# Gather, expert, scatter: large and small experts in turns, a fixed order of POOL's transfers, and two tails in one output tile

## The chip, the cores and the metric

The kernel runs on one core of a Trainium2 chip. The metric is the time of one execution on the device in microseconds (us); lower is better. Beside the times there is a profiled execution, from which every row below is taken. Engines: PE (matrix products; PEld is its weight load), DVE (vector), ACT (activation), POOL (here it issues indirect DMA transfers), SP (issues direct transfers).

## What is computed

One graph layer over 12,500 nodes with 256 features (a mean over neighbours with two normalisations, two linear maps), a mixture of 64 experts of which each node takes two, a normalisation over nodes, and a layer norm of the sum with the input:

```python
x = gc + (feats @ W_res + b_res)
logits = x @ Wg + bg
vals, idx = jax.lax.top_k(logits, TOP_K)          # TOP_K = 2, E = 64
gates = jax.nn.softmax(vals, axis=-1)
...
h1 = jax.nn.gelu(jnp.einsum('ecd,edh->ech', h, w1) + b1[:, None, :])   # D 256 -> H 512
h2 = jnp.einsum('ech,ehd->ecd', h1, w2) + b2[:, None, :]              # H 512 -> D 256
core = jnp.zeros((N, D), x.dtype).at[tok_s].add(g_s[:, None] * y_s)
y = x + core
...
return _layernorm(x + batch_normalised(y))
```

h holds, for each expert, the rows of x of the nodes that chose it (at most 1024). All products are in float32, which PE does in two passes.

## The kernel before

Three stages follow each other: the graph layer with the choice of experts (to about 2552 us), the experts (2552 to 3434 us), and the two normalisations. The change touches the expert stage alone.

Experts are ordered by how many nodes they have, largest first, and expert number i of this order has room for TOKENS[i]×16 rows. An expert's rows are cut into **parts** of at most four tiles of 128 rows: 83 parts and 241 tiles in all. The last tile of an expert, its **tail**, is often short. The order of parts is the smallest expert (number 63), then 0, 1, 2 and so on to 62.

For part q the program goes through these steps.

- `begin(q)`: for a new expert, SP loads its weights (1 MB, tile `w`, L1614) and bias (L1616) and DVE copies its lists of slots (L1762, L1764). Then POOL issues one indirect gather a tile, `xg` (L1638), of the rows of x and of what the gate needs; 16 buffers.
- `turned(q)`: DVE computes the gates of the part's tiles from the gathered rows (L1682), PE transposes the tiles into `xtp` (L1653), and DVE copies that to `xT` (L1658).
- `hidden`: PE's first products `hp` (L1667), and ACT's gelu into `h1` (L1671).
- `outputs`: for each tile, PE's second products `yp` (L1694; four j of 128 hidden units, each in two passes; two PSUM buffers), DVE adds the bias (L1699) and multiplies by the gate (L1700) into `yo` (6 buffers), and POOL issues a scatter that adds the rows of yo to z_d in memory (L1701).

The loop over q runs `hidden(q)`, `begin(q + 3)`, `turned(q + 1)`, `outputs(q)`. PE keeps this order as written. For the other engines a scheduler orders the instructions; each engine then works through its own order, and an instruction that waits holds up those behind it. POOL's gathers and scatters share one queue of transfers. The scatters of one expert may run side by side, since no node has an expert twice; those of different experts wait for each other where they meet the same tensor.

A second pass over all experts, under a condition that holds only when an expert has more rows than its room, is skipped with this data.

Of the kernel before, what the change touches and what calls it, by code (L numbers as in the profile page):

```python
# [19 lines left out]
P = 128  # L20
# [76 lines left out]
def last_node(g):  # L97
# [12 lines left out]
]  # L110
RPE = CAP // P
NSLOT = E * RPE
WROW = 2 * H + 4 * D + 4
# [8 lines left out]
def gnn_moe_kernel(  # L122
# [697 lines left out]
    with ExitStack() as stack:  # L820
# [780 lines left out]


    with ExitStack() as stack:
        wp = stack.enter_context(tc.tile_pool(name="w", bufs=3))
        one = stack.enter_context(tc.tile_pool(name="x_one", bufs=1))
        two = stack.enter_context(tc.tile_pool(name="x_two", bufs=2))
        ps1 = stack.enter_context(tc.tile_pool(name="x_ps1", bufs=1, space=PSUM))
        ps2 = stack.enter_context(tc.tile_pool(name="x_ps2", bufs=2, space=PSUM))

        REGS = 4  # L1610

        def load(e):
            w = wp.tile([P, WROW], F32, name="w")
# [5 lines left out]
        def overfull():  # L1619
# [8 lines left out]
            V.tensor_reduce(some, room, axis=AX.X, op=ALU.add)  # L1628
            V.tensor_copy(over_n, some)

        def gather(at, m):

            xg = []
            for k in range(0, m, P):
                r = min(P, m - k)
                k //= P
                g = two.tile([P, D2], F32, name="xg", bufs=16)
                GP.indirect_dma_start(  # L1638
                    out=g[:r],
                    out_offset=None,  # L1640
                    in_=x2_d,
                    in_offset=bass.IndirectOffsetOnAxis(ap=at[:r, 0, k : k + 1], axis=0),
                )
                xg.append(g[:r])
            return xg

        def turn(xg):

            xtp = ps1.tile([P, 2, 4 * P], F32, name="xtp")
            for k, g in enumerate(xg):  # L1650
                r = g.shape[0]
                for c in range(2):
                    T.transpose(  # L1653
                        xtp[:, c, k * P : k * P + r], g[:, c * P : (c + 1) * P], ident[:r, :r]
                    )
            m = k * P + r
            xT = two.tile([P, 2, 4 * P], F32, name="xT")
            V.tensor_copy(xT[:, :, :m], xtp[:, :, :m])  # L1658
            return xT
# [25 lines left out]
                )  # L1685
            return gate

        def outputs(w, bb, at, gate, h1, m, group):
            w2 = w[:, 2 * H : 2 * H + 4 * D].rearrange("p (c d) -> p c d", d=D)
            for k in range(-(-m // P)):  # L1690
                r = min(P, m - k * P)
                yp = ps2.tile([P, D], F32, name="yp")
                for j in range(4):
                    T.matmul(  # L1694
                        yp[:r], h1[:, j, k * P : k * P + r], w2[:, j],
                        start=j == 0, stop=j == 3,
                    )
                yo = two.tile([P, D], F32, name="yo", bufs=6)
                V.tensor_add(yo[:r], yp[:r], bb[:r])  # L1699
                V.tensor_scalar_mul(yo[:r], yo[:r], gate[:r, k : k + 1])  # L1700
                st = GP.indirect_dma_start(  # L1701
                    out=z_d,
                    out_offset=bass.IndirectOffsetOnAxis(
                        ap=at[:r, 1, k : k + 1], axis=0
                    ),
                    in_=yo[:r],
                    in_offset=None,
                    compute_op=ALU.add,
                )
                if group:  # L1710
                    tc.declare_no_dep(st.ins, group=group, reason="no node has an expert twice")
                    tc.add_to_no_dep_group(group, st.ins)


        parts = []
        for i in [E - 1, *range(E - 1)]:
            n = -(-TOKENS[i] * TU // P)
            k = -(-n // 4)
            b = 0
            for j in range(k):  # L1720
                m = (n - b + k - j - 1) // (k - j)
                parts.append((i, b, min(m * P, TOKENS[i] * TU - b * P)))
                b += m
        AHEAD = 3
        xg, given = {}, {}

        def begin(q):
            i, b, m = parts[q]
            if b == 0:
                k = 0 if i == E - 1 else i % REGS  # L1730
                if k == 0:
                    n = 1 if i == E - 1 else min(REGS, E - 1 - i)
# [14 lines left out]
                    given["regs"] = regs, columns  # L1747
                regs, columns = given["regs"]
                columns_of[i] = columns[k]
                sort_slots(i, 0)  # L1750
                if q >= AHEAD:
                    sort_slots(i, 1)
                given[i] = load(regs[k])
            xg[q] = gather(table(q), m)

        columns_of = {}

        def sort_slots(i, which):

# [6 lines left out]
        def table(q):  # L1766
            i, b, m = parts[q]
            return sorted_[:, :, i * RPE + b : i * RPE + b + 4]

        def turned(q):  # L1770
            i, b, m = parts[q]
            gate[q] = gates_of(xg[q], snd_sorted[:, i * RPE + b : i * RPE + b + 4])
            return turn(xg.pop(q))

        gate = {}
        snd_sorted = one.tile([P, NSLOT], F32)
        with tc.manual_schedule(engines={mybir.EngineType.PE}):
            for q in range(AHEAD):
                begin(q)
            V.scalar_tensor_tensor(free, node, 0.0, spread, op0=ALU.is_equal, op1=ALU.mult)  # L1780
            V.tensor_tensor(slot[:, 1], free, slot[:, 0], op=ALU.add)
            for i in sorted({parts[q][0] for q in range(AHEAD)}):
                sort_slots(i, 1)
            xT = turned(0)
            for q, (i, b, m) in enumerate(parts):
                if q >= 6 and q % 4 == 2 and (q - 6) // 4 < len(LOADS):
                    t0, n = LOADS[(q - 6) // 4]
                    r = rows(t0)
                    nc.sync.dma_start(xs[:r, t0 : t0 + n], part_of(x, t0, n))
                h1 = hidden(given[i][0], xT, m)  # L1790
                if q + AHEAD < len(parts):
                    begin(q + AHEAD)
                if q + 1 < len(parts):
                    xT = turned(q + 1)
                outputs(*given[i], table(q), gate.pop(q), h1, m, f"expert{i}")
                if q == 16:
                    overfull()


        with tc.If(nc.values_load(over_n[0:1, 0:1]) > 0):  # L1800
            for a in range(NT):
                r = rows(a)
                again = two.tile([P, D], F32, name="yo", bufs=6)
                nc.sync.dma_start(again[:r], x2_d[a * P : a * P + r, :D])
                nc.sync.dma_start(z_d[a * P : a * P + r], again[:r])
            with tc.For_i(0, E, 1) as e:
                w, bb = load(e)
                at = two.tile([P, 2, RPE], I32, name="at")
                V.tensor_copy(at, slot[:, :, bass.ds(e * RPE, RPE)])
                second = two.tile([P, RPE], F32, name="second")  # L1810
                V.tensor_copy(second, snd[:, bass.ds(e * RPE, RPE)])
                for b in range(0, RPE, 4):
                    ab = at[:, :, b : b + 4]
                    g = gather(ab, 4 * P)
                    gb = gates_of(g, second[:, b : b + 4])
                    outputs(w, bb, ab, gb, hidden(w, turn(g), 4 * P), 4 * P, None)


    with ExitStack() as stack:
# [191 lines left out]
```

## Time and profile before

| | us |
|---|---|
| median of 3 runs | 3605.96 (3599.64 to 3620.2) |
| profiled execution | 3578.72 |
| its span | 3576.8 |
| PE busy | 2531.0 (71%) |
| DVE busy | 1800.6 (50%) |
| ACT busy | 798.8 (22%) |
| POOL busy | 2175.5 (61%) |

The span covers all stages; the expert stage is its last quarter but for the normalisations. A row of the timeline gives start, duration, engine, line, operation, output and inputs, and in brackets the idle time of the engine just before with what ended it ("<-DMA xg" is the landing of a gather, "<-issue" nothing that the profile shows). A row of a group gives count, busy time, mean ns of one, and idle time by what ended it. POOL's busy time is that of issuing; the transfer goes on after it.

### The profile page before, as it was taken

Reading aid. Unit: us, or ns where it says so; the run is one execution under the profiler, and the core shown is the slowest. Engines: PE = TensorE matmul, PEld = TensorE weight load, DVE = VectorE, ACT = ScalarE, POOL = GpSimd, SP = SyncE. Lnnn points to the kernel's source line nnn. Section 1 sums busy time; section 2 is a strip of 40 time slices with the busy share of each in tenths; the row PEclk is TensorE's granted clock in tenths of the full one; section 3 lists DMA queues with packets and bytes.
Section 4 is the critical chain, followed back from the end, with each engine's and each line's share of the span. In section 5 each row is a group of like instructions: output and inputs, shape, how many; then the busy total and the mean of one; then the engine's idle time right before and its main releaser. Section 6 shows DMA issues by size and latency. Waiting matters only on the chain. (4 is left out here: it accounts for less than half of the span.)

```text
span 3576.8 us, 40049 instructions
## 1 busy us (share of the span) xinstructions
PE 2531.0 (71%) x11797; PEld 1893.4 (53%) x11797; DVE 1800.6 (50%) x7368; ACT 798.8 (22%) x1975; POOL 2175.5 (61%) x2095
## 2 busy tenths in 40 slices
PE   2526075566776667676766666677699999999966
PEld 2415043455555555554555444454377876677856
DVE  3729454355555465655555435467543333333358
ACT  2416301122111122212221111111111221122246
POOL 7250776666666666666666666665367777777610
PEclk6657566778887878897878777788899999999988
DMA  8450853444554555555544444444555666676764
GB/s 259 128 189 6 309 203 95 158 145 144 143 150 146 141 147 168 146 147 157 155 144 122 142 117 122 119 135 124 159 115 122 134 135 146 155 177 173 197 196 144
DMA packets 313919, 538.03 MB, mean 150 GB/s; under 512 B 47274, under 2 KB 233102, under 8 KB 305502
## 3 DMA queue, kind: packets, MB, share of 16 engines
q0 software_dynamic: 119360, 266.30, 28.9%
q1 hardware_dynamic: 180795, 256.19, 23.0%
q10 hardware_dynamic: 13539, 12.90, 1.2%
q8 instruction: 97, 1.59, 0.2%
q14 instruction: 128, 1.05, 0.1%
HBM read 431.02 MB, written 105.28 MB: 150 GB/s over the span
## 5 line engine op out<-in xcount | busy, mean ns | idle before, releaser
L938 POOL DMA_INDIRECT ring<-h_d,src_col x1416 | 1372.4, 969 | 711.8 <-issue 387.2
L952 PE MATMUL p<-ring,o 128*128 128x258 f32 x2832 | 902.0, 450 | 213.2 <-issue 89.7
L952 PEld LDWEIGHTS p<-ring,o 128*128 128x128 f32 x2832 | 600.4, 224 | 389.2 <-issue 214.9
L930 DVE TENSOR_SCALAR o<-lane,rel 128x128 f32<-128x128 f32 x1416 | 356.1, 297 | 402.7 <-remote 160.3
L1701 POOL DMA_INDIRECT z_d<-yo,tables x241 | 375.0, 1556 | 129.8 <-issue 58.0
L1694 PE MATMUL yp<-w,h 128*128 128x256 f32 (+7 forms) x1928 | 436.3, 381 | 0.8 <-DVE tables L1762 0.8
L1667 PE MATMUL hp<-xT,w 128*128 128x384 f32 (+22 forms) x1328 | 392.3, 449 | 9.4 <-issue 9.4
L1694 PEld LDWEIGHTS yp<-w,h 128*128 128x128 f32 (+7 forms) x1928 | 336.8, 179 | 71.0 <-issue 7.6
L1638 POOL DMA_INDIRECT xg<-x_d,tables x241 | 234.3, 972 | 183.7 <-PE xtp L1653 88.2
L1671 ACT ACTIVATE h<-hp,w 128x384 f32<-128x384 f32 (+21 forms) x332 | 178.7, 539 | 682.0 <-PE hp L1667 673.1
L1667 PEld LDWEIGHTS hp<-xT,w 128*128 128x128 f32 x1328 | 248.0, 192 | 134.1 <-issue 61.0
L1506 ACT ACTIVATE again<-again,factor 128x256 f32<-128x256 f32 x180 | 82.4, 501 | 670.3 <-issue 363.2
L986 ACT COPY s<-p 128x258 f32<-128x258 f32 x118 | 43.8, 371 | 814.8 <-PE p L952 450.0
L1658 DVE COPY xT<-xtp 128x672 f32<-128x672 f32 (+21 forms) x83 | 70.8, 853 | 305.6 <-PE xtp L1653 297.2
L1699 DVE TENSOR_TENSOR yo<-yp,bb 128x256 f32<-128x256 f32 (+7 forms) x241 | 102.0, 423 | 224.1 <-PE yp L1694 154.2
L285 POOL DMA_INDIRECT early<-in_x,src_col x130 | 135.0, 1038 | 102.4 <-DMA early_d<-early 56.3
L567 PE MATMUL deg<-o_hi,o_lo 128*128 128x98 bf16 x1254 | 107.3, 254 | 122.8 <-issue 83.8
L1481 PE MATMUL q<-r_out,tables 128*128 128x98 f32 x360 | 66.8, 315 | 150.4 <-DVE tables L1489 55.9
L1027 PE MATMUL q<-ident,s 128*128 128x128 f32 x236 | 58.9, 337 | 158.0 <-DVE tables L1489 67.5
L222 DVE TENSOR_TENSOR o_hi<-lane_b,hi 128x2450 bf16<-128x2450 bf16 (+1 forms) x67 | 95.1, 1419 | 145.8 <-remote 106.2
L565 ACT ACTIVATE s_lo<-lane_b,nb 128x128 bf16<-128x128 bf16 x396 | 121.8, 388 | 192.9 <-remote 126.7
L567 PEld LDWEIGHTS <-o_lo 128*128 128x128 bf16 x1254 | 87.5, 125 | 140.1 <-issue 91.2
(367 smaller groups left out, 3503.5 us busy)
## 6 DMA issues: line engine op xcount, KB each, us to landing
w<-in_wpack SPq DMA_DIRECT2D x64, 1026.0 KB
again<-early_d SPq DMA_DIRECT2D x90, 256.0 KB
ring<-h_d,src_col POOLq DMA_INDIRECT x1416
early_d<-early SPq DMA_DIRECT2D x65, 256.0 KB
tables<-h_d SPq DMA_DIRECT2D x104, 128.0 KB
acc<-acc_d SPq DMA_DIRECT2D x14, 896.0 KB
acc<-in_x SPq DMA_DIRECT2D x12, 1024.0 KB
x_d<-y SPq DMA_DIRECT2D x47, 258.0 KB
```

The costliest lines, as they stand in the source:

```text
L285: GP.indirect_dma_start(out=t[:, c % 2], out_offset=None, in_=x, in_offset=bass.IndirectOffsetOnAxis(ap=src_col[:, MC + c : MC + c + 1], a ...
L565: S.activation(s_lo[:, i], lane_b, AF.Sign, bias=nb[:, k - k0, i : i + 1])
L567: T.matmul(deg, o_lo[:, i], o_hi[:, i], start=c + i == 0, stop=False)
L930: o_last[u] = V.tensor_scalar(o_of[u][:, j], lane, rel[:, c : c + 1], None, op0=ALU.is_equal)
L938: i = GP.indirect_dma_start(out=r[:, k, :D], out_offset=None, in_=h_d, in_offset=bass.IndirectOffsetOnAxis(ap=src_col[:, c : c + 1], axis=0),)
L952: i = T.matmul(p_of[g], o_of[v][:, n], r[:, k], start=j == 0, stop=j == GR - 1)
L1638: GP.indirect_dma_start(out=g[:r], out_offset=None, in_=x2_d, in_offset=bass.IndirectOffsetOnAxis(ap=at[:r, 0, k : k + 1], axis=0),)
L1667: T.matmul(hp[:, :m], w1[:, c, j * P : (j + 1) * P], xT[:, c, :m], start=c == 0, stop=c == 1,)
L1671: S.activation(h1[:, j, :m], hp[:, :m], AF.Gelu, bias=w[:, 2 * H + 4 * D + j : 2 * H + 4 * D + j + 1],)
L1694: T.matmul(yp[:r], h1[:, j, k * P : k * P + r], w2[:, j], start=j == 0, stop=j == 3,)
L1699: V.tensor_add(yo[:r], yp[:r], bb[:r])
L1701: st = GP.indirect_dma_start(out=z_d, out_offset=bass.IndirectOffsetOnAxis(ap=at[:r, 1, k : k + 1], axis=0), in_=yo[:r], in_offset=None, c ...
```

## The change

Four things change in the expert stage.

- **Order of experts.** Experts (or pairs, below) are sorted by their rows, and one from the large end and one from the small end are taken in turns. The weights of an expert are found by a register load for each expert, where consecutive ones came from one load of four. `w` has 4 buffers instead of 3, `yo` 10 instead of 6.
- **Pairs.** 17 pairs of experts are formed whose tails fit together into one tile of 128 rows: two tails of 33 to 64 rows (5 pairs), or one of up to 32 and one of 65 to 96 (12 pairs). The two tails' products go to one PSUM tile `yp`, in blocks of PE's columns, 64 wide in the first case and 32 wide in the second, and block by block for each j. DVE's add and multiply and POOL's scatter are still done for each tail. Of the pair's second expert the part with the tail comes first. Its scatters wait for those of the first expert.
- **POOL's order.** Gathers and scatters get dependencies that bind only the order of issue: a gather follows what was issued before it in the program, and so does a scatter, the scatters of one expert in a row being free among themselves. In a pair's step `begin(q + 3)` stands between the scatters of the two tails.
- **Tail gathers** bring at least 80 rows, and `turn` transposes and copies as many.

```diff
-        wp = stack.enter_context(tc.tile_pool(name="w", bufs=3))
+        wp = stack.enter_context(tc.tile_pool(name="w", bufs=4))
...
+        def in_order(i, group=None):
+            if "over" in issued:
+                return
+            if group is None or group != issued["group"]:
+                issued.update(group=group, before=issued["these"], these=[])
+            for j in issued["before"]:
+                tc.add_manual_dep(
+                    i.ins, j.ins.name,
+                    mybir.DependencyInfo(
+                        mybir.DependencyClass.NoSync, mybir.DependencyReason.SCHED_ONLY
+                    ),
+                    reason="gathers and scatters are issued in this order",
+                )
+            issued["these"].append(i)
...
-                r = min(P, m - k)
+                r = max(WHOLE, min(P, m - k))
...
-                GP.indirect_dma_start(
+                i = GP.indirect_dma_start(
...
+                in_order(i)
...
+        def products(yp, r, w, h1, a, j):
+            w2 = w[:, 2 * H : 2 * H + 4 * D].rearrange("p (c d) -> p c d", d=D)
+            T.matmul(yp, h1[:, j, a : a + r], w2[:, j], start=j == 0, stop=j == 3)
...
+        def add_to_nodes(yo, at, k, group):
...
+                for before in scatters.get(mate.get(group), []):
+                    tc.add_manual_dep(
+                        st.ins, before.ins.name,
+                        mybir.DependencyInfo(mybir.DependencyClass.Sync, mybir.DependencyReason.DATA),
+                        reason="a node can have both experts of a pair",
+                    )
+                scatters.setdefault(group, []).append(st)
+                in_order(st, group)
...
+        def pair_of_outputs(two_of):
+            yp = ps2.tile([P, D], F32, name="yp")
+            tails = [of[5] % P for of in two_of]
+            width = SIDE if min(tails) > BLOCK and max(tails) <= SIDE else BLOCK
+            starts = [0, max(SIDE, -(-tails[0] // BLOCK) * BLOCK)]
+            for j in range(4):
+                for start, r, (w, bb, at, gate, h1, m, group) in zip(starts, tails, two_of):
+                    for k in range(0, r, width):
+                        n = min(width, r - k)
+                        products(yp[start + k : start + k + n], n, w, h1, m - r + k, j)
+            todo = []
+            for start, r, (w, bb, at, gate, h1, m, group) in zip(starts, tails, two_of):
+                part_of_yp = slice(start, start + r)
+                yo = gated(yp[part_of_yp], r, bb[part_of_yp], gate, m // P)
+                todo.append(lambda yo=yo, at=at, m=m, group=group: add_to_nodes(yo, at, m // P, group))
+            todo[0]()
+            return todo[1]
...
+        order = [E - 1]
+        while units:
+            order += units.pop(0)
+            if units:
+                order += units.pop()
+        order.append(E - 2)
         parts = []
-        for i in [E - 1, *range(E - 1)]:
+        for i in order:
...
-                if q + AHEAD < len(parts):
+                if q not in pair_at and q + AHEAD < len(parts):
                     begin(q + AHEAD)
                 if q + 1 < len(parts):
                     xT = turned(q + 1)
-                outputs(*given[i], table(q), gate.pop(q), h1, m, f"expert{i}")
+                mine = (*given[i], table(q), gate.pop(q), h1, m, f"expert{i}")
+                if q in pair_at:
+                    rest = pair_of_outputs([kept.pop(pair_at[q]), mine])
+                    begin(q + AHEAD)
+                if q in pair_at or q in pair_at.values():
+                    if q not in pair_at:
+                        kept[q] = mine
+                    mine = (*mine[:5], m // P * P, mine[6])
+                if q in pair_at:
+                    rest()
+                    outputs(*mine)
+                else:
+                    outputs(*mine)
```

`gated` holds the add and the multiply of DVE, `add_to_nodes` the scatter, both as they were in `outputs`. SIDE is 64, BLOCK 32, WHOLE 80, and AHEAD is 3 in both kernels.

More of the change, by code (lines that the diff above doesn't have):

```diff
@@ L110, with blocks_of @@
 ]
+SIDE, BLOCK = P // 2, P // 4
+WHOLE = SIDE + 16
+def blocks_of(r):
+    return -(-r // BLOCK)
+PAIR_OF = {}
+for _k in ((2, 2), (1, 3), (1, 1)):
+    _open = []
+    for _i, _n in enumerate(TOKENS[: E - 2]):
+        _u = blocks_of(_n * TU % P)
+        if _u not in _k or _i in PAIR_OF or _i in PAIR_OF.values():
+            continue
+        _mate = [_j for _j, _v in _open if (_v, _u) in (_k, _k[::-1])]
+        if _mate:
+            PAIR_OF[_mate[0]] = _i
+            _open = [_o for _o in _open if _o[0] != _mate[0]]
+        else:
+            _open.append((_i, _u))
 RPE = CAP // P
@@ L1655, in turn @@
                     )
-            m = k * P + r
             xT = two.tile([P, 2, 4 * P], F32, name="xT")
@@ L1686, in gates_of, with gated, outputs @@
             return gate
-        def outputs(w, bb, at, gate, h1, m, group):
+        def products(yp, r, w, h1, a, j):
             w2 = w[:, 2 * H : 2 * H + 4 * D].rearrange("p (c d) -> p c d", d=D)
-            for k in range(-(-m // P)):
+            T.matmul(yp, h1[:, j, a : a + r], w2[:, j], start=j == 0, stop=j == 3)
+        def gated(yp, r, bb, gate, k):
+            yo = two.tile([P, D], F32, name="yo", bufs=YO)
+            V.tensor_add(yo[:r], yp, bb)
+            V.tensor_scalar_mul(yo[:r], yo[:r], gate[:r, k : k + 1])
+            return yo[:r]
+        def add_to_nodes(yo, at, k, group):
+            r = yo.shape[0]
+            st = GP.indirect_dma_start(
+                out=z_d,
+                out_offset=bass.IndirectOffsetOnAxis(ap=at[:r, 1, k : k + 1], axis=0),
+                in_=yo,
+                in_offset=None,
+                compute_op=ALU.add,
+            )
+            if group:
+                tc.declare_no_dep(st.ins, group=group, reason="no node has an expert twice")
+                tc.add_to_no_dep_group(group, st.ins)
+                for before in scatters.get(mate.get(group), []):
[3 more added lines that the diff above has]
+                        reason="a node can have both experts of a pair",
+                    )
+                scatters.setdefault(group, []).append(st)
+                in_order(st, group)
+        scatters = {}
+        mate = {f"expert{j}": f"expert{i}" for i, j in PAIR_OF.items()}
+        def outputs(w, bb, at, gate, h1, m, group, ks=None):
+            for k in ks or range(-(-m // P)):
                 r = min(P, m - k * P)
@@ L1693, in outputs @@
                 for j in range(4):
[L1694 to L1709, printed above, removed]
@@ L1710, in outputs @@
-                if group:
-                    tc.declare_no_dep(st.ins, group=group, reason="no node has an expert twice")
-                    tc.add_to_no_dep_group(group, st.ins)
+                    products(yp[:r], r, w, h1, k * P, j)
+                add_to_nodes(gated(yp[:r], r, bb[:r], gate, k), at, k, group)
+        def pair_of_outputs(two_of):
[15 more added lines that the diff above has]
+            return todo[1]
@@ L1715, in gnn_moe_kernel @@
+        units = []
+        for i in range(E - 2):
+            if i not in PAIR_OF.values():
+                units.append([i, PAIR_OF[i]] if i in PAIR_OF else [i])
+        units.sort(key=lambda u: -sum(TOKENS[i] for i in u))
+        order = [E - 1]
[4 more added lines that the diff above has]
+        order.append(E - 2)
         parts = []
-        for i in [E - 1, *range(E - 1)]:
+        for i in order:
             n = -(-TOKENS[i] * TU // P)
@@ L1728, in begin @@
             i, b, m = parts[q]
[L1729 to L1732, printed above, removed]
+            if i not in given:
+                if i not in columns_of:
+                    n = 1
+                    at = order.index(i)
+                    while n < REGS and order[at : at + n + 1] == [*range(i, i + n + 1)]:
+                        n += 1
                     _, regs = nc.values_load_multi_w_load_instructions(
@@ L1746, in begin @@
                     )
-                    given["regs"] = regs, columns
-                regs, columns = given["regs"]
-                columns_of[i] = columns[k]
+                    for k in range(n):
+                        columns_of[i + k], reg_of[i + k] = columns[k], regs[k]
                 sort_slots(i, 0)
```

28 lines of the change are left out of this document (19 added, 9 removed).

## The prediction

> **What bounds the kernel now.** I read the windows of the expert stage first, to see which engine is never idle there, then the groups by line, then the waits, and last the timelines of single tiles. Columns of the windows: stretch, its length, then busy time of PE, PEld, DVE, ACT and POOL with instruction counts, granted clock, DMA share, GB/s.
>
> ```profile
> 2560.00:2600.00 40.00, 29.27 (x107) 19.77 (x107) 21.69 (x146) 6.24 (x10) 26.82 (x26) 0.84 0.61 178
> 2600.00:2900.00 300.00, 300.00 (x1301) 227.09 (x1300) 114.57 (x362) 63.45 (x116) 213.19 (x168) 1.00 0.59 125
> 2900.00:3200.00 300.00, 300.00 (x1262) 212.41 (x1261) 103.87 (x278) 59.56 (x104) 213.43 (x170) 1.00 0.66 153
> 3200.00:3410.00 210.00, 210.00 (x975) 164.13 (x974) 74.38 (x202) 45.83 (x93) 138.53 (x108) 1.00 0.74 187
> ```
>
> From 2600 to 3410 PE is busy for 300.00 of 300 and 210.00 of 210 us, at full clock: PE sets the pace. POOL is next, 213 of 300, and its rows leave out the gap between two issues, so it is fuller than that. The stage runs from the first gather to the end of the last scatter:
>
> ```profile
> 2552.15 1.11 POOL L1638 DMA_INDIRECT xg<-x_d,tables  x1 [40.81 <-DVE tables L1762]
> ...
> 2584.75 1.63 POOL L1701 DMA_INDIRECT z_d<-yo,tables  x1 [4.24 <-DVE tables L1762]
> 2586.68 1.41 POOL L1701 DMA_INDIRECT z_d<-yo,tables  x1 [0.30 <-issue]
> ...
> 3432.79 1.44 POOL L1701 DMA_INDIRECT z_d<-yo,tables  x1 [0.30 <-issue]
> ```
>
> That is 2552.15 to 3434.23, 882 us. The groups of this stretch (count, busy us, mean ns of one, idle before):
>
> ```profile
> L1694 PE MATMUL yp<-w,h 128*128 128x256 f32 (+7 forms) x1928 | 436.3, 381 | 0.8 <-DVE tables L1762 0.8
> L1701 POOL DMA_INDIRECT z_d<-yo,tables x241 | 375.0, 1556 | 129.8 <-issue 58.0 <-DVE yo L1700 26.5 <-DVE gate L1682 23.8
> L1638 POOL DMA_INDIRECT xg<-x_d,tables x239 | 232.3, 972 | 142.6 <-PE xtp L1653 88.2 <-issue 38.7 <-PE yp L1694 13.0
> L1699 DVE TENSOR_TENSOR yo<-yp,bb 128x256 f32<-128x256 f32 (+7 forms) x241 | 102.0, 423 | 224.1 <-PE yp L1694 154.2 <-issue 38.2 <-DMA xg<-x_d,tables 16.4
> L1700 DVE TENSOR_SCALAR yo<-yo,gate 128x256 f32<-128x256 f32 (+7 forms) x241 | 89.2, 370 | 8.2
> L1658 DVE COPY xT<-xtp 128x672 f32<-128x672 f32 (+21 forms) x83 | 70.8, 853 | 305.6 <-PE xtp L1653 297.2 <-remote 8.3
> L1682 DVE SCALAR_TENSOR_TENSOR gate<-snd_sorted,xg 128x1 f32<-128x1 f32 (+7 forms) x241 | 39.4, 215 | 13.7 <-DMA xg<-x_d,tables 10.9
> ```
>
> POOL issues 241 gathers (two of them before this view's window) and 241 scatters. With the 0.30 us that stands as the idle time between two issues in nearly every POOL row, its work is 241×(0.972+0.30) + 241×(1.556+0.30) = 306.6 + 447.3 = **754 us** out of 882. This holds as long as nobody waits for a gather that POOL has only just issued. Today hardly anyone does: in the gates' row only 10.9 us of DVE's idle time ends on the landing of xg.
>
> **The column blocks.** Two tiles of products and a tile alone, on PE:
>
> ```profile
> 3116.46 0.82 PE L1653 MATMUL xtp<-ident,xg 128*128 128x128 f32 x6
> 3117.12 7.18 PE L1694 MATMUL yp<-w,h 128*128 128x256 f32 x32
> 3124.22 1.24 PE L1667 MATMUL hp<-xT,w 128*128 128x384 f32 x3
> ```
>
> Four output tiles, 32 instructions, take 3124.22 − 3117.12 = 7.10 us, so 0.222 an instruction and 1.78 a tile (8 instructions: four j, two passes). The last of the four has only 16 rows and still its 8 instructions: a tail costs like a whole tile. There are 17 pairs, so today's price is 17×2×1.78 = 60.5 us. Five pairs become two blocks of 64 columns each, 8 products or 16 instructions; twelve become four blocks of 32, 16 products or 32 instructions. The trace has no two blocks side by side, so bounds: if blocks fully overlap, a pair costs one tile, 17×1.78 = 30 us saved; if none do, the twelve cost 32 instructions instead of 16, 12×3.55 = 43 us lost and the five nothing. Between them: both passes of a block must add up in order, so overlap may reach only neighbours; then the five save 9 and the twelve nothing. I take 9, the value of the fewest assumptions, and keep −30 and +43.
> The Trainium skill ("TensorE: Matmul & The Clock Gate", Part 3: Packing small matmuls — row/col tiling) measured 2.38× for three column tiles side by side, which is near the first bound. No run here shows it; by it the 32 instructions of a pair would take 7.1/2.38 = 3.0 us instead of 3.55, an estimate, and the twelve would save 7 us more.
> Gathers of tails now bring at least 80 rows. No row shows an 80-row gather apart from the rest; all stand between 0.97 on average and the 1.11 above, so 24 such tails cost 0 to 3 us of POOL; I take nothing.
>
> **Turns, the fourth weight buffer, ten yo.** These reorder and give room; no instruction of PE, ACT or DVE's arithmetic becomes more, only some 47 register loads on DVE, since the experts are no longer four in a row. The profile doesn't count those as busy. Bounds 0 and 47×0.30 = 14 us, if each costs what an issue gap costs; DVE is busy 114 of 300 us, which hides them except ahead of a gate or yo. I take 0.
>
> **The forced order on POOL** decides. In the built kernels' instruction order (G a gather, s a scatter, number the part, ×n how many):
>
> ```
> before  G0..G5 (22 gathers) s0 s0 G6 G6 G6 G7 s1×4 ... s6×3 G13 G13 G14 s7 ...
> after   G0..G3 (13 gathers) s0 ... s5 s5 G9×3 s6×3 G10 G10 s7×3 G11×3 s8 ...
> ```
>
> Before, gathers run some seven parts ahead of the scatters; after, three. Neither kernel changes where DVE has its gates: the program computes those of a part early, and DVE's order has the gates of part q+3 ahead of the yo of part q, often with the copy xT of part q+1 between. The gate of a tile needs its gather landed. So after the change each turn is a closed loop: scatters of q−1, gathers of q+3, their landing, their gates on DVE, xT, yo of q, scatters of q. Queued behind a waiting gate on DVE are that xT (for which PE's next hidden layer waits) and yo (for which PE's two yp banks wait): PE is stopped with it. Counting in the order, of 80 runs of scatters that follow a gather, **63 need exactly the gather just ahead of them**, and 38 of the 63 have an xT between; before, the nearest such distance is 9 POOL instructions, mostly 17 and more.
>
> What one turn costs. Landing of a gather, from two of which DVE's gate had nothing else to wait for:
>
> ```profile
> 2565.76 0.95 POOL L1638 DMA_INDIRECT xg<-x_d,tables  x1 [0.30 <-issue]
> 2567.02 0.95 POOL L1638 DMA_INDIRECT xg<-x_d,tables  x1 [0.30 <-issue]
> ...
> 2568.78 0.22 DVE L1682 SCALAR_TENSOR_TENSOR gate<-snd_sorted,xg 128x1 f32<-128x1 f32 x1 [0.29 <-DMA xg<-x_d,tables]
> 2569.96 0.22 DVE L1682 SCALAR_TENSOR_TENSOR gate<-snd_sorted,xg 128x1 f32<-128x1 f32 x1 [0.96 <-DMA xg<-x_d,tables]
> ```
>
> 2569.96 − (2567.02 + 0.95) = 1.99 after the end of the issue, 2.07 for the other: 2.0. Then a gate 0.22, yo's add 0.42 and multiply 0.37, less the 0.30 that POOL idles anyway: 2.71 us, 63 times = 171; and 38 xT of 0.853 = 32. Together **203 us** in which POOL issues nothing.
> The Trainium skill ("DMA: Bandwidth & Descriptors", Anatomy of one DMA — SWDGE (gpsimd) path) gives 2.0 us and bytes over 436 GB/s per transfer, an estimate of 2.3 us for 128 rows of 258 floats, counted from the issue; the rows have 2.94 and 3.02. By the page each turn is 0.7 us shorter and the sum 43 us less. The trace decides.
>
> Start: 13 gathers end at about 2568.8, and the first scatter can't come before 2584.75, where it is today since PE and DVE get there no sooner: **16 us** of POOL idle (4.24 today, after 20 gathers in this stretch).
>
> Weight loads. A scatter that lands alone, and one after which a weight load was issued:
>
> ```profile
> 3211.30 0.34 SPq L1614 DMA_DIRECT2D w<-in_wpack  x1
> ...
> 3213.19 1.43 POOL L1701 DMA_INDIRECT z_d<-yo,tables  x1 [0.31 <-issue]
> ...
> 3221.22 1.63 POOL L1701 DMA_INDIRECT z_d<-yo,tables  x1 [1.83 <-DMA z_d<-yo,tables]
> ...
> 3432.79 3.70 DMA z_d<-yo,tables
> ```
>
> The first took 3221.22 − 3213.19 = 8.03 us to land, the other (from the chain that ended last) 3.70: the load holds POOL's transfers up by 4.3 us. 64 loads come one each 15 us or so. A landing falls into such a stretch with a chance of 4.3/15 and loses half of it: 0.62 us, 63 times = **39 us**. Bounds: 0, if loads always come after the landing, and 63×2.15 = 135.
>
> The second expert's first scatter in a pair now waits for its mate's. Two to four gathers (1.27 each) stand between, which cover the 3.70 − 1.56 = 2.1 us that are left after the mate's issue: nothing; uncovered, 17×2.1 = 36.
>
> **Sum.** 754 + 203 + 16 + 39 = 1012 us for a stage that takes 882: +130. What PE saves in the pairs doesn't come off, as PE waits. Against the profiled execution of 3578.72 us (span 3576.8) that makes 3709; the median of the runs shown, 3605.96, lies 27 above the profiled one, so **3736**. Its own range: without the loads' 39 and the xT's 32, 3665; with the loads at 135, 3832.
>
> **Rivals.** The loop decides where a turn is longer than PE's work on it. PE has 882/80 = 11.0 us a turn, POOL 754/80 = 9.4, so from a wait of 1.6 us a turn on; I have 3.2.
> (a) The loop stays hidden and the blocks overlap fully: the other side of the line. Landing, gate and yo would have to fit into 1.2 us beside 10.6 of PE. For it: POOL has 128 us to spare now, and both orders are only issue orders. Against it: the landing alone took 2.0. Time: 3606 − 30 = **3576**.
> (b) Hidden loop, neighbours overlap only: 3606 − 9 = **3597**. For and against as before, with the passes' order for it.
> (c) Hidden loop and the blocks do not overlap, so the change doesn't do what it says: 3606 + 43 = **3649**. Against: PE's array is addressed by columns already for today's tails, but no row shows two at once.
> (d) The loop binds and the loads come mostly in the landing, or PE's 43 us add to the turn: 3832 and above.
>
> **How the numbers follow.** Loop near my price, 3665 to 3832: 0.75. (a) 0.11, (b) 0.07, (c) and a half-hidden loop between 3624 and 3665 0.05, (d) 0.02. A measurement of this kernel can tell about 0.5%, 18 us, from no change: (a) is faster, (b) the same, the rest slower. 3635 to 3830 leaves out (a), (b) and little of the rest, 2 in 10.
>
> **What would show it.** In the profile after: PE no longer full in the windows of the expert stage, 0.85 to 0.92 of each; DVE's gate or yo groups with over 100 us of idle time ended by the landing of xg, against 10.9 and 16.4 now; scatters whose row says 2.5 us or more of idle on a gate or yo, directly behind a gather; the last scatter near 3560. Wrong: PE full from 2600 on, gates without waits on xg; or a stretch at the start or the end, not spread over all turns, that holds the loss. For the blocks: the PE time between the first and last product of a pair, 1.8 if all overlap, 3.6 or 7.1 if not.

## The result, and the profile after

| | before | changed |
|---|---|---|
| median of 6 runs, us | 3607.52 (3595.25 to 3622.89) | 3827.26 (3819.05 to 3853.95) |
| ratio, 95% interval | 1 | 1.0619 (1.0575 to 1.0663) |
| profiled span, us | 3576.8 | 3826.9 |

Slower by 220 us. The way was forecast (+130, 3736 us), the size was not; 3827 lies just under the range's upper end of 3830.

Two measures serve for all that follows. The **stage** is the time from the first gather's start to the last scatter's end; the graph stage ahead of it runs the same instructions in all kernels, yet its length differs by some 45 us between profiled executions, so a stage tells more than a total. **POOL's wait** is the idle time of the scatters' group less 241×0.30 = 72.3 us of issue gaps.

The windows of the changed kernel, in the same columns as before:

```profile
2700.00:2800.00 100.00, 82.58 (x383) 62.76 (x381) 26.34 (x73) 16.90 (x33) 57.09 (x46) 0.91 0.54 124
3100.00:3200.00 100.00, 75.53 (x341) 54.26 (x342) 25.22 (x71) 14.76 (x28) 51.19 (x42) 0.85 0.48 109
3500.00:3600.00 100.00, 78.60 (x349) 58.47 (x348) 25.29 (x70) 15.02 (x28) 57.97 (x48) 0.88 0.56 136
3640.00:3680.00 40.00, 40.00 (x170) 29.69 (x169) 11.62 (x28) 8.23 (x15) 17.35 (x12) 1.00 0.38 54
```

PE is busy for 76 to 83 of 100 us, POOL issues for 51 to 58 of 100 us instead of 71, and no other engine has more to do: a closed loop of waits. It ends at about 3640, with the last gathers; from there PE is full. The granted clock is 0.85 to 0.91 where it was 1.00. The groups say what the wait is:

```profile
L1739 POOL DMA_INDIRECT z_d<-yo,tables x241 | 374.9, 1556 | 428.4 <-DVE yo L1734 359.1 <-issue 35.8 <-DVE yo L1733 16.1
L1721 DVE SCALAR_TENSOR_TENSOR gate<-snd_sorted,xg 128x1 f32<-128x1 f32 (+3 forms) x241 | 51.6, 218 | 568.8 <-DMA xg<-x_d,tables 565.7 <-issue 0.9
L1706 PE MATMUL hp<-xT,w 128*128 128x384 f32 (+21 forms) x1328 | 418.3, 471 | 74.9 <-DVE xT L1697 73.8 <-DVE gate L1721 1.1
L1729 PE MATMUL yp<-w,h 128*128 128x256 f32 (+5 forms) x2120 | 445.6, 400 | 134.7 <-DVE yo L1733 134.6
```

DVE's gates wait 565.7 us for gathers to land, against 10.9 before. Behind them PE waits 134.6 for yo to free its yp banks and 73.8 for xT, and POOL's scatters 359.1 for yo. POOL's wait is 428.4 − 72.3 = 356 us, against 129.8 − 72.3 = 57 before. The stage:

```profile
2572.67 1.08 POOL L1677 DMA_INDIRECT xg<-x_d,tables  x1 [42.58 <-DVE tables L1854]
...
2588.78 0.91 POOL L1677 DMA_INDIRECT xg<-x_d,tables  x1 [0.30 <-issue]
2596.34 1.63 POOL L1739 DMA_INDIRECT z_d<-yo,tables  x1 [6.64 <-DVE yo L1734]
...
3683.29 1.44 POOL L1739 DMA_INDIRECT z_d<-yo,tables  x1 [0.30 <-DVEq L1905]
```

2572.67 to 3684.73, 1112 us instead of 882, which is 754 of POOL's work and 356 of its wait. One common turn, from the timelines of POOL and DVE:

```profile
2833.32 0.96 POOL L1677 DMA_INDIRECT xg<-x_d,tables  x1 [0.30 <-issue]
2837.79 1.62 POOL L1739 DMA_INDIRECT z_d<-yo,tables  x1 [3.51 <-DVE yo L1734]
...
2836.57 0.22 DVE L1721 SCALAR_TENSOR_TENSOR gate<-snd_sorted,xg 96x1 f32<-96x1 f32 x1 [0.90 <-DMA xg<-x_d,tables]
2836.71 0.41 DVE L1733 TENSOR_TENSOR yo<-yp,bb 128x256 f32<-128x256 f32 x1
2837.15 0.35 DVE L1734 TENSOR_SCALAR yo<-yo,gate 128x256 f32<-128x256 f32 x1
```

The gather's issue ends at 2834.28, the landing lets the gate start 2.29 us later, add and multiply follow, and the scatter starts 3.51 us after the issue ended. That is the chain of the prediction, link by link. In a turn with a pair, the scatter of the first tail waits another way, which the prediction did not price (POOL, then DVE, then PE):

```profile
3131.78 1.62 POOL L1739 DMA_INDIRECT z_d<-yo,tables  x1 [3.05 <-DVE yo L1734]
3141.78 1.45 POOL L1739 DMA_INDIRECT z_d<-yo,tables  x1 [8.38 <-DVE yo L1734]
...
3128.14 0.22 DVE L1721 SCALAR_TENSOR_TENSOR gate<-snd_sorted,xg 128x1 f32<-128x1 f32 x1 [6.38 <-DMA xg<-x_d,tables]
3128.27 0.98 DVE L1697 COPY xT<-xtp 128x800 f32<-128x800 f32 x1
...
3129.31 8.54 PE L1706 MATMUL hp<-xT,w 128*128 128x400 f32 x16 [3.05 <-DVE xT L1697]
3138.22 7.30 PE L1729 MATMUL yp<-w,h 128*32 128x256 f32 x56
```

xT had stood behind a waiting gate, PE's hidden layer behind xT, the pair's tile behind that, and POOL had no gather to issue: 8.38 us idle between two scatters. The 16 instructions of 400 columns took 8.54 us; in the kernel before, at full clock:

```profile
3110.99 5.64 PE L1667 MATMUL hp<-xT,w 128*128 128x400 f32 x16
```

### The profile page after: what moved, and what is told of

The parts are those of the page before. It is cut to its first block, busy times and chain, and to the rows that moved or that the text cites. A ratio compares the mean times of both kernels' runs of the same rounds, so it can differ in the third digit from the quotient of the medians.

```text
span 3826.9 us, 40289 instructions
## 1 busy us (share of the span) xinstructions
PE 2554.4 (67%) x11920; PEld 1906.7 (50%) x11989; DVE 1794.1 (47%) x7368; ACT 798.1 (21%) x1975; POOL 2173.2 (57%) x2095
## 5 line engine op out<-in xcount | busy, mean ns | idle before, releaser
L1739 POOL DMA_INDIRECT z_d<-yo,tables x241 | 374.9, 1556 | 428.4 <-DVE yo L1734 359.1
L1729 PE MATMUL yp<-w,h 128*128 128x256 f32 (+5 forms) x2120 | 445.6, 400 | 134.7 <-DVE yo L1733 134.6
L1706 PE MATMUL hp<-xT,w 128*128 128x384 f32 (+21 forms) x1328 | 418.3, 471 | 74.9 <-DVE xT L1697 73.8
L1729 PEld LDWEIGHTS yp<-w,h 128*128 128x128 f32 (+5 forms) x2120 | 334.5, 179 | 215.1 <-DVE yo L1733 147.5
L1706 PEld LDWEIGHTS hp<-xT,w 128*128 128x128 f32 x1328 | 263.6, 204 | 212.5 <-DVE xT L1697 80.6
L1721 DVE SCALAR_TENSOR_TENSOR gate<-snd_sorted,xg 128x1 f32<-128x1 f32 (+3 forms) x241 | 51.6, 218 | 568.8 <-DMA xg<-x_d,tables 565.7
L1733 DVE TENSOR_TENSOR yo<-yp,bb 128x256 f32<-128x256 f32 (+6 forms) x241 | 101.1, 420 | 116.5 <-PE yp L1729 114.8
```

The costliest lines, as they stand in the source:

```text
L1706: T.matmul(hp[:, :m], w1[:, c, j * P : (j + 1) * P], xT[:, c, :m], start=c == 0, stop=c == 1,)
L1729: T.matmul(yp, h1[:, j, a : a + r], w2[:, j], start=j == 0, stop=j == 3)
L1733: V.tensor_add(yo[:r], yp, bb)
L1739: st = GP.indirect_dma_start(out=z_d, out_offset=bass.IndirectOffsetOnAxis(ap=at[:r, 1, k : k + 1], axis=0), in_=yo, in_offset=None, compu ...
```

## The experiments

Each kernel was measured beside the kernel before. Beside some of them that kernel took 3155 us instead of 3601 to 3608, since its graph stage was shorter then. So kernels are compared by their ratio to the kernel before measured beside them, and by stages, each read from one profiled execution. Ratios over different times of the kernel before don't compare directly: the 1.0671 without pairs, over 3155 us, is a loss of 211 us, the 1.0619 of the changed kernel one of 220.

| kernel | ratio, 95% interval | stage, us | POOL's wait, us |
|---|---|---|---|
| before | 1 | 882 | 57 |
| changed | 1.0619 (1.0575 to 1.0663) | 1112 | 356 |
| without the forced order | 0.9991 (0.9950 to 1.0032) | 870 | 109 |
| forced order alone | 1.0539 (1.0476 to 1.0602) | 1075 | 319 |
| late gates | 0.9962 (0.9933 to 0.9990) | 859 | 101 |
| gathers first in pair turns | 1.0648 (1.0588 to 1.0707) | 1123 | 367 |
| without pairs | 1.0671 (1.0647 to 1.0696) | 1089 | 333 |

**Without the forced order.**

```diff
         def in_order(i, group=None):
-            if "over" in issued:
-                return
+            return
```

> The changed kernel without the forced order on POOL; turns, pairs, four weight buffers and 80-row gathers stay. In its instruction order 22 gathers stand ahead of the first scatter again and no run of scatters needs one of the 9 POOL instructions ahead of it. Loop theory (scatters, gathers, landing, gates on DVE, yo, scatters): the loss of 220 us goes altogether, PE is full in the expert stage and the pairs' saving shows: 3565 to 3610 us; idle time of DVE's gates that ends on xg falls from 566 to under 40 us. Rival (the turns, the register loads or the pairs' tile cost it, whatever POOL's order is): over 3700.

Measured: 3600.76 us, the ratio within noise of 1. The wait of the gates on xg fell to 17.7 us:

```profile
L1738 POOL DMA_INDIRECT z_d<-yo,tables x241 | 375.1, 1556 | 180.8 <-issue 53.4 <-DVE yo L1733 45.9 <-DMA z_d<-yo,tables 36.9
L1720 DVE SCALAR_TENSOR_TENSOR gate<-snd_sorted,xg 128x1 f32<-128x1 f32 (+3 forms) x241 | 39.8, 214 | 21.5 <-DMA xg<-x_d,tables 17.7 <-issue 1.7
```

All of the loss went with the forced order; turns, register loads and pairs cost nothing that shows. The gain of the pairs, though, hardly shows in the total either; the scatters' 36.9 us on the landing of z_d, the wait for a mate, are new.

**The forced order alone.** `in_order` as in the change, put into the kernel before:

```diff
+                in_order(i)
                 xg.append(g[:r])
...
                     tc.add_to_no_dep_group(group, st.ins)
+                    in_order(st, group)
```

> The kernel before with the forced order on POOL alone: no turns, no pairs, three weight buffers. Its instruction order has 80 runs of scatters, 78 of which need the gather just ahead of them. Loop theory: POOL's work of 754 us, 80 turns of about 3.3 us as measured in the changed kernel (264), 16 at the start and some 15 at the end make a stage of 1050 instead of 882 us: 3740 to 3800. It is below the changed kernel by what that loses between two scatters in pair turns (about 66 us). Rival (the loss comes from turns or pairs): 3590 to 3625.

Measured: 3803.94 us, a touch above the range, stage 2596.73 to 3672.20.

```profile
L1720 POOL DMA_INDIRECT z_d<-yo,tables x241 | 376.0, 1560 | 391.6 <-DVE yo L1719 308.3 <-issue 34.1 <-DVE yo L1718 26.0
```

So one part of the four makes 193 of the 230 us. Its wait of 391.6 − 72.3 = 319 us is 303 directly behind gathers, in 80 turns: 3.79 us a turn. (The 3.3 expected was the mean over the changed kernel's 80 runs, 17 of which hardly wait behind gathers.)

**Late gates.** POOL's order stays; DVE's gates of part q come behind the multiplies of part q−2:

```diff
+                for j in muls.get(q, []):
+                    tc.add_manual_dep(
+                        i.ins, j.ins.name,
+                        mybir.DependencyInfo(
+                            mybir.DependencyClass.NoSync, mybir.DependencyReason.SCHED_ONLY
+                        ),
+                        reason="gates come behind an earlier part's yo",
+                    )
...
+            gate[q] = gates_of(xg[q], snd_sorted[:, i * RPE + b : i * RPE + b + 4], q - 2)
```

`muls` holds the multiplies of each part; `gates_of` is given q−2.

> The changed kernel with POOL's order as it is; only DVE's gates of part q are put behind the multiplies of part q-2 in the order of issue. Every run of scatters then needs a gather at least 8 POOL instructions back. Loop theory with the gates' place on DVE as its decisive link: nearly all of the loss goes, 3565 to 3640 us. Rival (three parts are too few gathers ahead, so that POOL's order costs by itself): over 3740, with the waits moved from the gates to PE's transposes or to the scatters.

Measured: 3591.38 us. The wait on the landing shrinks to a tenth, though POOL issues the very same order:

```profile
L1750 POOL DMA_INDIRECT z_d<-yo,tables x241 | 375.8, 1559 | 173.6 <-issue 60.5 <-DVE yo L1745 59.3 <-DMA z_d<-yo,tables 19.0
L1724 DVE SCALAR_TENSOR_TENSOR gate<-snd_sorted,xg 128x1 f32<-128x1 f32 (+3 forms) x241 | 41.7, 213 | 60.6 <-DMA xg<-x_d,tables 56.8 <-issue 3.2
```

The two links are needed together: the order on POOL and the gates ahead of yo on DVE. Take either away and the loss is gone. The rival fell: with late gates, gathers three parts ahead cost nothing that shows.

**The forced order alone, with late gates.** The two edits before, together in the kernel before.

> The kernel before with the forced order on POOL, and with DVE's gates of part q behind the multiplies of part q-2: no turns, no pairs. No run of scatters needs one of the 8 gathers and scatters ahead of it. Theory (the order costs only by way of the gates' place on DVE): the 193 us that the order alone cost in the stage go, 3590 to 3625 us, stage 875 to 900. Rival (the order costs by itself where no pairs give PE slack): 3640 or more.

Measured: ratio 0.9981 (0.9971 to 0.9990), 3148.83 against 3155.14 us, stage 877. As the theory had it: without turns and pairs, too, the order costs only by way of the gates.

**Gathers first in pair turns.**

```diff
-                if q not in pair_at and q + AHEAD < len(parts):
-                    begin(q + AHEAD)
+                if q + AHEAD < len(parts):
+                    begin(q + AHEAD, q not in pair_at)
...
                     rest = pair_of_outputs([kept.pop(pair_at[q]), mine])
-                    begin(q + AHEAD)
+                    load_for(parts[q + AHEAD][0])
```

With False as its second argument `begin` leaves the weight load to `load_for`.

> The changed kernel with the gathers of part q+3 ahead of the pair's scatters in a pair's step, as in other steps; the weight load stays where it was. The number of turns that need the gather just ahead stays 63. Theory: the 91 us that POOL idles between two scatters in the changed kernel come from the 15 to 17 pair turns, in which it has no gather left to issue while PE is still at the second expert's hidden layer; with gathers there, 50 to 70 us of them go: 3755 to 3785. Rival (these waits are the same loop's and only move to behind the gathers): 3810 to 3840.

Measured: 3827.33 us. My theory fell. The waits ahead of the first tails shrank to 26 us, now behind gathers, and 68 us came ahead of the second tails, which follow their mates at once and wait for them to land:

```profile
3131.90 1.49 POOL L1739 DMA_INDIRECT z_d<-yo,tables  x1 [2.96 <-DVE yo L1734]
3138.37 1.32 POOL L1739 DMA_INDIRECT z_d<-yo,tables  x1 [4.98 <-DMA z_d<-yo,tables]
```

In the changed kernel 16 waits of over 2 us between two scatters, 69 us in all beyond the gaps, stand ahead of first tails, and 15 us behind gathers ahead of second ones. The stage is 11 us longer.

**Half of the gathers before, half between.** On top of the edit before:

```diff
-            xg[q] = gather(table(q), m)
+            if weights:
+                xg[q] = gather(table(q), m)
+            else:
+                xg[q] = gather(table(q), m, 0, -(-m // P) // 2)
...
                     load_for(parts[q + AHEAD][0])
+                    some = parts[q + AHEAD][2]
+                    xg[q + AHEAD] += gather(table(q + AHEAD), some, -(-some // P) // 2)
```

> The changed kernel (early gates, fixed order on POOL), with half of the gathers of part q+3 ahead of the first tail's scatter of a pair's step and the other half between the two tails. 63 runs of scatters still need the gather just ahead. In the changed kernel 69 us of POOL's idle time stand ahead of first tails; with all gathers moved ahead of them 68 us stood ahead of the second tails, on the landing of the mate's scatter. Theory (two separate waits, each of which one or two gathers can cover in part): both together fall to 15 to 45 us, and the stage to 1060 to 1095 from 1112 us, 3775 to 3810 us. Rival (the time of a pair's turn is set by the loop over gates, xT and PE's hidden layer, wherever the gathers stand): waits move to the runs behind gathers, stage 1105 to 1125, 3815 to 3845 us.

Measured: ratio 1.0748 (1.0730 to 1.0766), 238 us over the 3156 of the kernel before beside it, stage 1113 us.

```profile
L1739 POOL DMA_INDIRECT z_d<-yo,tables x241 | 375.0, 1556 | 428.1 <-DVE yo L1734 338.8 <-issue 42.8 <-DVE yo L1733 26.1
```

The scatters' idle time is 428.1 us, in the changed kernel 428.4. The waits between two scatters did fall, from 91 to 22 us, but those behind gathers rose from 264 to 333. The rival stands: the loop sets how long a pair's turn takes, and where POOL idles in it depends on where its instructions stand.

**Without pairs.**

```diff
-for _k in ((2, 2), (1, 3), (1, 1)):
+for _k in ():
```

> The changed kernel without pairs: the turns, the fixed order on POOL, four weight buffers and 80-row gathers stay. All 80 runs of scatters need the gather just ahead. Loop theory, with the pair turns as the place of the 91 us between two scatters: POOL's work 754, 80 turns of 3.3 to 3.8 us (264 to 303) and about 16 between scatters at the end: a stage, from the first gather to the end of the last scatter, of 1034 to 1075 instead of 1112 us, 3750 to 3795 us in all, though the pairs' saving on PE is gone. Rival (pairs save their 29 us also here, and the waits between scatters are the loop's): 3830 to 3860.

Measured (two runs): stage 1089 us, 14 above the range's upper end, POOL's wait 333. Between the theories: the waits between scatters went (91 to 21), those behind gathers rose to 311, as all 80 turns now pay there, 3.89 us each. The 17 pair turns cost 23 us more than the turns that stand in their place.

**What the pairs save.** The edit without pairs on top of late gates, first apart from late gates with pairs, then beside them:

> The changed kernel with late gates and without pairs: against the same with pairs (3591 us, stage 859) it gives what the pairs save where no loop covers it. Theory (blocks of columns overlap fully, 1.82 to 1.86 us for a pair's 32 instructions in the changed kernel's trace instead of 3.55): 17 pairs save 29 us, so this stage is 880 to 892 and the time 3610 to 3625. Rival (the pairs' own waits on PE and for the mate's scatters give most of it back): 855 to 870, time as with pairs.

> The changed kernel with late gates once more, now on the same chip and in the same rounds as that without pairs (last of these runs) and with other POOL orders, since the pairs' saving can only be read from a direct comparison. Theory (pairs shorten PE's work by 30 us, and what is left of POOL's waits gives part of it back): stage 855 to 865, 0 to 15 us faster than without pairs. Rival (nothing is gained by pairs): the same as without within 3 us.

> Late gates without pairs, beside the same with pairs. PE was full here and its stage 864.5 us. Theory: PE's 864 us stay, so 0 to 15 us slower than with pairs. Rival: the same within 3 us.

Measured: without pairs 0.9956 (0.9942 to 0.9970) with a stage of 864.5, and again 0.9972 (0.9944 to 1.0000) with 864.6; with pairs again 0.9964 (0.9943 to 0.9985) with 858.6. The first expectation of 880 to 892 missed. In time the rival of the last two held: 3597.67 us with pairs, 3595.34 without, no difference. 6 us in the stage is all that the pairs bring. From 50 us after the first gather on, 750 us, with pairs and without:

```profile
2634.88:3384.88 750.00, 734.74 (x3551) 557.17 (x3550) 274.04 (x786) 159.61 (x301) 543.96 (x430) 0.99 0.68 159
```

```profile
2643.41:3393.41 750.00, 750.00 (x3324) 564.81 (x3324) 270.36 (x778) 158.78 (x297) 541.72 (x428) 1.00 0.69 158
```

Without pairs PE never stops. With them it idles 15 us, which takes back most of 6 + 15 = 21 us that its work has become shorter, an estimate. The profile puts 9.0 us of this idle time down to DVE, which has to free a bank of yp, and 6.1 to gathers that land late.

**Late gates without the forced order.** The edits of the first and the third experiment together.

> The changed kernel without the forced order on POOL and with DVE's gates behind the multiplies of part q-2. With neither link of the loop left it should stand within 10 us of the better of the two kernels that lack one link each (3591 and 3601): 3580 to 3610, stage 855 to 872. If the waits that were left without the forced order (POOL's scatters that wait for a mate's landing, 37 us) set its stage, it stays at 869; if the gates did, it falls to 859 or below.

> Late gates without the forced order, once more beside the others. Its profiled execution had the shortest stage (852 us), with PE done 17 us before the last scatter, but its times spread over 30 us. Theory (POOL is its bound: 754 us of work and some 96 of waits): stage 848 to 860 again. Whether its time stands below that of late gates in the fixed order is open: within 10 us of it either way.

Measured: 0.9980 (0.9963 to 0.9997) with a stage of 852, then 0.9982 (0.9948 to 1.0015) with 884. The stage didn't repeat, so the second expectation missed, and single stages of this kernel can't be compared to within 32 us (late gates gave 859.3 and 858.6, those without pairs 864.5 and 864.6). In both profiled executions the last scatter ends 18 to 19 us behind the last product, with late gates in the fixed order 3 to 6; that POOL sets the stage here is suggested by this, not shown.

**Late gates, gathers split in pair turns.** Both edits together.

> Late gates, and in a pair's step half of the gathers of part q+3 ahead of the first tail's scatter and the other half between the two tails, so that POOL has something to issue while PE is at the pair's tile and while the first tail's scatter lands. Theory (PE's remaining idle time of some 16 us in this stage comes from POOL's waits in pair turns): PE is full, stage 845 to 856, 3 to 12 us below late gates alone. Rival (those waits come from elsewhere, such as gathers that land late behind weight loads): no difference within 3 us.

Measured: 0.9946 (0.9922 to 0.9971), 3590.38 us, with late gates alone 3597.67 beside it; the intervals overlap. The stage is 870, not 845 to 856, and PE is busy for 729.59 of the same 750 us: the theory that PE would be full doesn't hold, and why POOL's and DVE's work leaves PE idle there with pairs is open. All versions with late gates stand 0.2 to 0.5% below the kernel before, the smaller of these differences at the edge of the noise.

## Why the prediction was right and wrong

- **The loop.** Right in each link: the place (gates ahead of yo), the landing after the end of an issue (2.0 forecast, 2.29 in the turn shown), and the count. In the changed kernel's trace 63 of the 80 runs of scatters behind gathers have a gate that waited for the last gather ahead of their yo, 38 of them with an xT between. Shown by taking away either link. The rivals with a hidden loop fell.
- **The price of a turn.** (203 + 39)/63 = 3.84 us with the loads' share. In the changed kernel the 63 turns have 249 us, 6 of them in the first one; the other 62 have 3.92 each. The order alone has 3.79, the kernel without pairs 3.89: right. The loads' share comes out too: in 19 of the 63 turns over 0.05 MB moved on SP's queue (weights and biases) between the start of the last gather's issue and its gate, and there the landing took 3.64 us from the end of the issue, in the other 44 turns 1.93. That is 19×1.71 = 33 us, an estimate, against 39; rival (d), loads in most of the turns, fell with it.
- **The step that failed: "63 need exactly the gather just ahead of them", with the other 17 turns at no price.** Those are the pair turns. The scatter behind the gathers there doesn't need the last gather, but the first tail's scatter ahead of them needs PE's tile, PE needs xT, and xT stands behind the same gates on DVE. I had named that queue (xT, then PE's hidden layer, then the banks) and then summed POOL's waits as if only yo stood in it. POOL's wait of 356 us, 98 more than the 258 forecast, divides in the trace into 249 in the 63 turns (242 and 16 for the start forecast), 69 ahead of first tails, 15 ahead of second tails, 15 after the last gather, from 3640 on, and 8 in small waits between scatters. So the pair turns, forecast at nothing, make 84 us, or 4.9 a turn, and the end, which the sum left out, 15. That the 69 come by way of the gates is shown by late gates, which bring POOL's waits between scatters from 91 to 18 us while POOL's order stays; moving the gathers did not shorten the pair turns. That the time still fell into the range was luck: its upper end came from weight loads at 135 us, not from pair turns.
- **The mate's landing.** "Nothing" was too little, by 15 us. Gathers do stand between, but in eight of the 17 pair turns they didn't cover the landing. The profile puts only 3.4 us down to it and most of the rest to gates; a scatter doesn't need the gate that ended just before it, and the trace's semaphore events have the mate landed 0.8 to 0.9 us ahead of the second tail in all eight. One of them (POOL, then DVE):

```profile
3037.68 1.45 POOL L1739 DMA_INDIRECT z_d<-yo,tables  x1 [6.82 <-DVE yo L1734]
...
3044.87 1.41 POOL L1739 DMA_INDIRECT z_d<-yo,tables  x1 [3.18 <-DVE gate L1721]
...
3040.19 0.35 DVE L1734 TENSOR_SCALAR yo<-yo,gate 128x256 f32<-128x256 f32 x1
```

  yo was ready at 3040.54, the mate landed at 3044.06, 6.38 us after its start instead of 3.70. From 3037.7 to 3040.8 packets moved on SP's queue alone (0.94 MB; a weight load was issued at 3036.19), none on POOL's. Uncovered I gave 36 us; with the gathers moved away it was 68.
- **The column blocks.** Mis-sized in the safe direction: I took neighbours only, and they overlap almost fully. In the changed kernel 48 instructions, 16 of them of whole tiles, took 5.41 us from start to next start:

```profile
2700.41 5.57 PE L1729 MATMUL yp<-w,h 128*32 128x256 f32 x48
2705.82 0.49 PE L1706 MATMUL hp<-xT,w 128*128 128x384 f32 x1
```

  Less 16×0.222 that leaves 1.86 us for a pair's 32, not 7.1: 3.8 times as fast. A pair in two blocks of 64 comes out alike (3568.22 to 3573.64, 32 instructions less 16 of whole tiles: 1.87 us for 16, not 3.55). The Trainium skill ("TensorE: Matmul & The Clock Gate", Part 3: Packing small matmuls — row/col tiling) measured 2.38 times for three column tiles. The four blocks here did better, and the measurement decides. That the saving wouldn't come off while PE waits was right.
- **Turns, register loads, padding, yo buffers** at nothing: right as far as the changed kernel's total can tell (ratio 0.9991 without the order), where the pairs are in it too. Beside each other, both with the fixed order, late gates and no pairs, the kernel with these four took 3142.68 us and a stage of 864.5, the one without them 3148.83 and 877: together they save some 6 us, hardly clear of the noise (the intervals of the two ratios end at 0.9970 and begin at 0.9971).
- **The start.** 13 gathers and 6.64 us of idle instead of 16: POOL waited less, since the first scatter came 24 us after the first gather and not 33. (The kernel before issues 22 gathers ahead of its first scatter, not 20; no term rests on that.)
- **The signs.** They came, and stronger than said: PE was busy for 76 to 83% of the windows, not 85 to 92, and the last scatter began at 3683, not near 3560 (the stage itself began 20 us later).

## What to carry to other kernels

Before fixing an order of issue on one engine, follow each instruction through the queues of all engines that it feeds: an order that is harmless by itself closes a loop where another engine has a wait for its newest transfer ahead of the work that lets it go on. When such a loop is found, every turn pays, those too in which the wait shows on another engine; count turns, not visible waits. Here either repair works: to undo the order (ratio 0.9991), or to move the early wait back on its own queue and keep the order (0.9962).

## What the runs showed that was not expected

After a wait PE runs at about half speed for a while: the first whole tile after 7.73 us of idle took 3.42 us to the next start, against 1.78. The granted clock of these 3.42 us is 0.52. For the hidden layer of the pair turn shown above, 8.54 us instead of 5.64, it is 0.66, and for the same layer in the kernel before 1.00.

```profile
2657.49 3.58 PE L1729 MATMUL yp<-w,h 128*128 128x256 f32 x8 [7.73 <-DVE yo L1733]
2660.91 1.40 PE L1706 MATMUL hp<-xT,w 128*128 128x208 f32 x7
```

The graph stage of the same instructions ended 2552 to 2597 us after the start in some profiled executions and at about 2131 in others, while the expert stage of one kernel was 864.5 and 864.6 us in the two. What makes the graph stage shorter is open.
